# Joining the pairs of 128-column products in every step of an attention kernel: 50 fewer matmul calls

## The chip, the cores and the metric

The kernel runs on one core of a Trainium2 chip. The metric is the device time of one execution in microseconds (us), lower is better. Before the change it is 1023.34 us, the median of three runs (1022.62 to 1023.46).

## The reference, cut to what matters

```python
x: (64, 128, 512)   attn_bias: (16, 128, 128)   mask: (64, 128)   null_kv: (2, 64)     # float32
xn = layernorm(x, g_in)
q = (xn @ Wq).reshape(b, n, 16, 64).transpose(0, 2, 1, 3) * 64 ** -0.5
kv = xn @ Wkv                                   # one head of keys and values for all 16 query heads
k, v = kv[..., :64], kv[..., 64:]
k, v = null key ahead of k, null value ahead of v
sim = einsum('bhid,bjd->bhij', q, k) + bias     # causal and key mask
attn = softmax(sim, axis=-1)
out = einsum('bhij,bjd->bhid', attn, v)         # <- the products that the change joins
out = layernorm(out.transpose(0, 2, 1, 3).reshape(b, n, 1024) @ Wo, g_out)
return x + out
```

All is float32. A float32 matmul runs as two passes on TensorE (PE), each a weight load and a matmul, so one call in the code is four instructions on that engine.

## The kernel before, in words

64 batch elements are worked off in 32 pairs. The order of all work is written out by hand (`manual_schedule`): what stands first in the code stands first in its engine's stream. A step `d` is `turn(d)` and a body. `turn(d)` makes the scores of pair `d` (elements `a`, `b`), the attention-weighted values of the pair before (`p` and `p + 1`, with `p = 2d - 2`), and starts the softmax of `a`; the body has the key, query and output projections and the rest of the softmax. Steps 1 to 29 call `turn`, with `body` in steps 1 to 3 and `body_full` from 4; steps 30 to 32 call `turn_end`, which the change leaves alone.

On PE a step is three stretches: the scores (L780, 64 calls on 64x64 tiles of the array, into `sc_*` and `ps`), the values (L911, into `po`), and the body, mostly calls of 128x128 weights and 128 or 256 columns, which begins with `pkv` (L404). The values of one element are products of 32 keys: each of four groups of 32 queries (`s`) has its own 32 rows of the array, and each half of the heads (`r`) its own 64 columns, so eight tiles of the array work side by side. Causality leaves a group of queries only some blocks of keys. `sb` holds the transposed weights, six blocks of 32 by 32; of these `values` goes through four turns: the first has two blocks of a group in one call (256 columns), the next three have one each (128 columns). The argument `wide` names the groups (1 and 3) whose second and third turn are joined into one call of 256 columns:

```python
WIDE = (1, 3)
for turn in range(len(turns[0])):
    for s in range(NQ):
        j, to, n = turns[s % 2][turn]
        if s in wide and j == 1:
            if turn == 2:
                continue
            n = 2
        for r in range(2):
            nc.tensor.matmul(po[s][rows, to : to + n], vr[...], sb[quad, slots, ...], ...)
```

Without `wide` an element has 32 calls, with `WIDE[1:]` (group 3 alone) 30, with `WIDE` 28. In two steps from step 4 on, one of even and one of odd number, PE has 1536 instructions, its separate waits on semaphores counted. The results go from four tiles `po` in PSUM to `oT` by ScalarE (L930).

Of the kernel before, what the change touches and what calls it, by code (L numbers as in the profile page):

```python
# [17 lines left out]
def kernel(  # L18
# [515 lines left out]
    def token_sum(g, k):  # L534

        xS[g, k] = gp.tile([P, GB // 2, HK, N], FP, tag=f"xS{k}", name=f"xS{k}_{g}", bufs=1)
        lo, hi = xT[g][:, 0 : GB // 2], xT[g][:, GB // 2 :]
        b11, b12 = lo[:, :, lo_k], hi[:, :, lo_k]
        b21, b22 = lo[:, :, hi_k], hi[:, :, hi_k]
        p, m = {  # L540
            1: (b12, b11),
            2: (b22, xS.get((g, 1))),
            3: (b22, b12),
            4: (b21, xS.get((g, 2))),
        }[k]
        nc.gpsimd.tensor_tensor(xS[g, k], p, m, ALU.subtract)
# [182 lines left out]
    def mask_neg(g):  # L729
        m8 = m8s.pop(g).rearrange("p (t j) -> p t j", t=GB)  # L730
        for keys, m in ((LK, m8[:, :, 0:NL]), (UK, m8)):
            nc.scalar.activation(
                mneg[:, :, keys], m, AF.Identity, bias=neg, scale=-NEG
            )
# [3 lines left out]
    def bias_add(b, parts=(slice(0, ROW),)):  # L738
        g, t = divmod(b, GB)
        if b < B - 1:  # L740
            S[b] = sp.tile([P, R8, ROW], FP, tag="s", name=f"s_{b}", bufs=3)
        else:
            S[b] = hp.tile([P, R8, ROW], FP, tag="xb", name=f"s_{b}", bufs=1)
        for keys in parts:
            nc.gpsimd.tensor_tensor(  # L745
                S[b][:, :, keys],
                biasp[:, :, keys],
                mneg[:, t, keys]
                .unsqueeze(1)
                .broadcast_to([P, R8, keys.stop - keys.start]),  # L750
                ALU.add,
            )
# [12 lines left out]
    def scores(b, hf, tiles=None):  # L765
        g, t = divmod(b, GB)
        nk = N if hf == 1 else NL
        if tiles is None:
            whole = ps_s.tile([P, 2, NF * nk], FP, tag="s", name=f"ps_{b}_{hf}")
            whole = whole.rearrange("p r (f j) -> p r f j", f=NF)  # L770
            home = [whole[:, r] for r in range(2)]
            pss[b, hf] = whole
        else:
            home = rooms(b, hf, tiles)
            pss[b, hf] = home
        for f in range(NF):
            for r in range(2):
                rows = slice(r * DH, (r + 1) * DH)
                for u in range(2):
                    nc.tensor.matmul(  # L780
                        home[r][u * DH : (u + 1) * DH, f, :],
                        qT[g, f // 2, t // 2][rows, f % 2, t % 2, hf, u],
                        kT[rows, 0 : nk // Q, t, :],
                        start=True,
                        stop=True,
                    )
# [3 lines left out]
    def scores_add(b, hf):  # L790
        sv = S[b][:, :, KEYS[hf]].rearrange("p (r f) j -> p r f j", r=2)
        pv = pss.pop((b, hf))
        if isinstance(pv, list):
            for r in (1, 0):
                nc.vector.tensor_tensor(sv[:, r], pv[r], sv[:, r], ALU.add)  # L795
        else:
            nc.vector.tensor_tensor(sv, pv, sv, ALU.add)

    def scores_max(b, hf):
        if hf == 0:  # L800
            nmax[b] = small.tile([P, 2, R8], FP, tag="nmax", name=f"nmax_{b}")
        nc.vector.tensor_reduce(  # L802
            nmax[b][:, hf], S[b][:, :, WITH_NULL[hf]], AX.X, ALU.max, negate=True
        )

    def exps(b, hf, lo=0, hi=R8):
        if hf == 0 and lo == 0:
            rsum[b] = small.tile([P, 2, R8], FP, tag="rsum", name=f"rsum_{b}")
        for k in range(lo, hi):
            row = S[b][:, k, WITH_NULL[hf]]  # L810
            nc.scalar.activation(  # L811
                row,
                row,
                AF.Exp,
                bias=nmax[b][:, hf, k : k + 1],
                accum_out=rsum[b][:, hf, k : k + 1],
            )
# [38 lines left out]
    def values_rooms(  # L856
        p, rooms=((ps_q, "a"), (ps_w, "w"), (ps_y, "Y"), (ps_w, "w"))
    ):
        po = [
            pool.tile([P, 2, 2, NF, Q], FP, tag=tag, name=f"po_{p}_{s}")  # L860
            for s, (pool, tag) in enumerate(rooms)
        ]
        pos[p] = [t[:, :, 0] for t in po]
        pos[p + 1] = [t[:, :, 1] for t in po]
        return po
# [23 lines left out]
    WIDE = (1, 3)  # L889

    def values(b, wide=()):

        g, t = divmod(b, GB)
        sb = sbs.pop(b)
        po = pos[b]
        turns = (
            ((0, 0, 2), (1, 1, 1), (2, 1, 1), (3, 1, 1)),
            ((0, 0, 2), (1, 0, 1), (1, 1, 1), (2, 1, 1)),
# [8 lines that stand above are left out]
                quad = slice(s * Q, (s + 1) * Q)  # L907
                slots = slice(2 * to + j, 2 * to + j + 2 * n - 1, 2)
                for r in range(2):
                    rows = slice(r * DH, (r + 1) * DH)  # L910
                    nc.tensor.matmul(  # L911
                        po[s][rows, to : to + n],
                        vr[g][quad, t, PLACE[j], :],
                        sb[quad, slots, r * NF : (r + 1) * NF, :],
                        start=(turn == 0),
                        stop=True,
                        skip_group_check=(turn > 0),
                        tile_position=(s * Q, r * DH),
                    )
# [12 lines left out]
    def values_out(p, po):  # L932

        o = result_room(p)
        for s in range(NQ):
            u, i = divmod(s, 2)
            to = o[:, u].rearrange("p b f (s q) -> p s (b f) q", q=Q)[
                :, i : 4 - i : 3 - 2 * i
            ]
            add_null(to, po[s].rearrange("p s b f q -> p s (b f) q"), False)  # L940
# [148 lines left out]
    PAIRS = B // 2  # L1089
    late_T = []  # L1090

    def turn(d):

        a, b, p = 2 * d, 2 * d + 1, 2 * d - 2
        g = d // 2 + 1
        homes = (ps_y, "Y"), (ps_q, "a")
        if d == 1:
            homes = homes[::-1]
        scores(a, 0, (homes[0], (ps_w, "w")))
        scores(b, 0, (homes[1], (ps_w, "w")))  # L1100
        scores(a, 1)
        scores(b, 1, ((ps_y, "X"), (ps_q, "c")))
        scores_add(a, 0)
        scores_add(b, 0)
        scores_max(a, 0)
        scores_add(a, 1)
        scores_add(b, 1)
        po = values_rooms(p)
        steady = 3 < d < PAIRS - 2
        values(p, WIDE if steady else ())  # L1110
        values(p + 1, (WIDE if d % 2 else WIDE[1:]) if steady else ())
        if d % 2 and (d + 1) // 2 < NG:
            mask_neg((d + 1) // 2)
        bias_add(a + 2)
        if d % 2 == 0:
            token_sum(g, 1)
            token_sum(g, 2)
        exps(a, 0)
        values_out(p, po)
# [670 lines left out]
    for d in range(1, PAIRS - 2):  # L1790
        turn(d)
        (body_full if d > 3 else body)(d)
# [42 lines left out]
```

## Time and profile before

| What | Value |
|---|---|
| Median of three runs | 1023.34 us |
| The profiled execution's own time | 1022.45 us |
| Its span in the profile | 1020.6 us |
| PE busy (matmul) | 1012.9 us, 99% |
| PE weight loads busy | 902.0 us, 88% |
| VectorE, ScalarE, GpSimd busy | 860.8, 672.8, 775.0 us |
| Granted clock of PE | full in all 40 slices |
| Chain that ended last | PE 95%, ScalarE 2%, VectorE 1%, GpSimd 1% |
| Values (L911 into `po`) | 3700 matmuls |
| Instruction fetch of PE (queue q8) | 96 packets, 1.57 MB |

Rows of the timeline give the start of a group in us from the span's start, how long it lasts, the engine (PE matmul, PEld weight load), the line, the tiles (out <- in), the shape and the count. A row of windows gives the window, its length, the engine's busy time and the number of instructions in it, the granted clock, the DMA engines' busy share and GB/s. A row of waits says who waited for whom: us in total, times, longest. A row of a DMA queue gives packets, MB and the share of time of the 16 engines; in a window of some 0.02 us the share is over 100%, since a packet is counted whole where it starts.

### The profile page before, as it was taken

The numbers are of one execution on the slowest core, as the hardware profiler recorded it, in microseconds if no ns is written. First come the engines' busy times: TensorE is split into PE (matmuls) and PEld (weight loads), VectorE is DVE, ScalarE is ACT, GpSimd is POOL, SyncE is SP. The second block draws the span as 40 slices with busy tenths as digits, with TensorE's granted clock in tenths as the row PEclk, the third lists the DMA queues.
The fourth block names the chain that finished last, engine by engine and source line by source line (L and its number), as shares of the span: only waits on it lengthen the run. The fifth ranks groups of instructions, "written<-read, shape, count | busy, mean of one in ns | idle before, by whom it ended". The sixth has DMA issues, their size and how long they took to land.

```text
span 1020.6 us, 31143 instructions
## 1 busy us (share of the span) xinstructions
PE 1012.9 (99%) x12285; PEld 902.0 (88%) x12285; DVE 860.8 (84%) x1849; ACT 672.8 (66%) x2675; POOL 775.0 (76%) x621
## 2 busy tenths in 40 slices
PE   9999999999999999999999999999999999999997
PEld 9888888888888888888888888888888888888886
DVE  6877778888888988889888888888888888878787
ACT  5766677656677565686666776566765667856583
POOL 4997779678696876959768596785968769587686
PEclk9999999999999999999999999999999999999999
DMA  7415243151431425224152341514314152141221
GB/s 219 139 31 151 67 117 112 31 163 65 143 99 61 120 67 152 88 76 124 51 161 76 105 121 35 164 63 138 102 49 136 64 152 89 71 103 33 68 85 62
DMA packets 73833, 100.84 MB, mean 99 GB/s; under 512 B 32212, under 2 KB 36056, under 8 KB 71896
## 3 DMA queue, kind: packets, MB, share of 16 engines
q1 hardware_dynamic: 73392, 98.47, 32.3%
q8 instruction: 96, 1.57, 0.6%
q14 instruction: 49, 0.40, 0.1%
q10 hardware_dynamic: 296, 0.40, 0.1%
HBM read 63.19 MB, written 33.55 MB: 95 GB/s over the span
## 4 chain that ended last, share of the span: by engine, by line
PE 95%; ACT 2%; POOL 1%; DVE 1%; issue 0%; DMA 0%; POOLq 0%; DVEq 0%
PE pyX L998 20%; PE pa L603 13%; PE pi L697 11%; PE pyY L998 10%; PE po L911 8%; PE pkv L404 6%; PE pyw L998 5%; PE pc L603 4%; PE ps L780 3%; PE pq L499 3%; PE pa L554 2%; PE sc_X L780 2%; PE sc_Y L780 2%; PE pc L697 2%; ACT s L811 2%; PE pc L554 1%
## 5 line engine op out<-in xcount | busy, mean ns | idle before, releaser
L811 ACT ACTIVATE s<-s,nmax 128x65 f32<-128x65 f32 (+1 forms) x1024 | 370.9, 366 | 62.2 <-DVE nmax L802 62.2
L833 POOL TENSOR_TENSOR s<-s,rinv 128x512 f32<-128x512 f32 (+1 forms) x132 | 189.7, 1448 | 115.4 <-DVE rinv L829 112.9
L745 POOL TENSOR_TENSOR s<-biasp,mneg 128x1552 f32<-128x1552 f32 (+1 forms) x65 | 206.2, 3175 | 30.7 <-DVE s L795 21.2
L811 ACT ACTIVATION_READ_ACCUMULATOR s<-s,nmax 128x1 f32 x1024 | 194.5, 190 | 0.0
L725 DVE TENSOR_TENSOR qT<-pi,qT 128x128 f32<-128x128 f32 (+1 forms) x376 | 123.6, 340 | 35.9 <-PE pi L697 28.8
L1034 ACT COPY y<-pyX 128x256 f32<-128x256 f32 x29 | 10.8, 373 | 180.7 <-PE pyX L998 180.7
L802 DVE TENSOR_REDUCE nmax<-s 128x8 f32<-128x1032 f32 (+1 forms) x128 | 121.6, 950 | 0.1
L849 DVE STREAM_TRANSPOSE sb<-s 128x1536 f32<-128x1536 f32 (+1 forms) x68 | 113.6, 1674 | 2.1 <-POOL s L833 1.7
L998 PE MATMUL pyX<-wT,oT 128*128 128x256 f32 x464 | 109.7, 379 | 0.0
L998 PE MATMUL pyX<-wo,oT 128*128 128x256 f32 x464 | 109.7, 379 | 0.0
L978 POOL TENSOR_TENSOR oT<-oT 128x512 f32<-128x512 f32 x64 | 81.1, 1278 | 26.4 <-PE pyw L998 24.1
L998 PEld LDWEIGHTS pyX<-wT,oT 128*128 128x128 f32 x464 | 84.0, 190 | 9.2
L998 PEld LDWEIGHTS pyX<-wo,oT 128*128 128x128 f32 x464 | 84.0, 190 | 9.2
L911 PE MATMUL po<-sb,vr 32*64 32x128 f32 (+1 forms) x3700 | 86.2, 315 | 0.1
L911 PEld LDWEIGHTS po<-sb,vr 32*64 32x64 f32 x3700 | 74.8, 131 | 9.5 <-issue 5.3
L930 ACT ACTIVATE oT<-po,nv 128x512 f32<-128x512 f32 (+1 forms) x127 | 73.9, 660 | 0.4 <-PE po L911 0.4
L404 PE MATMUL pkv<-xT,wkv 128*128 128x256 f32 x256 | 63.3, 391 | 0.0
L998 PE MATMUL pyw<-wo,oT 128*128 128x256 f32 x256 | 60.5, 379 | 0.0
L998 PE MATMUL pyY<-wo,oT 128*128 128x256 f32 x256 | 60.5, 379 | 0.0
L998 PE MATMUL pyY<-wT,yS 128*128 128x256 f32 x256 | 60.5, 379 | 0.0
L614 ACT COPY qT<-pa 128x512 f32<-128x512 f32 x78 | 45.4, 582 | 17.7 <-PE pa L603 17.7
L404 PEld LDWEIGHTS pkv<-xT,wkv 128*128 128x128 f32 x256 | 46.2, 189 | 10.0 <-issue 4.8
(231 smaller groups left out, 2510.1 us busy)
## 6 DMA issues: line engine op xcount, KB each, us to landing
res<-in_x_dram SPq DMA_DIRECT2D x64, 256.0 KB
out_dram<-y SPq DMA_DIRECT2D x63, 256.0 KB
x<-in_x_dram SPq DMA_DIRECT2D x62, 256.0 KB
xd<-xb SPq DMA_DIRECT2D x14, 1024.0 KB
xT<-xd SPq DMA_DIRECT2D x56, 256.0 KB
vr<-vd SPq DMA_DIRECT2D x64, 128.0 KB
kT<-kT SPq DMA_DIRECT2D x32, 64.0 KB
vd<-vb SPq DMA_DIRECT2D x32, 64.0 KB
```

Of the source, the lines that this page charges most:

```text
L404: nc.tensor.matmul(pkv, wkv[:, kc, :], xT[g][:, t : t + 2, kc, :], start=(kc == 0), stop=(kc == KC - 1),)
L603: nc.tensor.matmul(prod[tag][:, i], w[:, kc, f * P : (f + 1) * P], t[:, :, kc, :], start=first, stop=(kc == HK - 1), skip_group_check=not ...
L697: nc.tensor.matmul(to, inner_w[k][i][:, h], inner_x[k, g][i], start=(i == 1), stop=True, skip_group_check=(i != 1),)
L725: nc.vector.tensor_tensor(o, p, o, ALU.add)
L745: nc.gpsimd.tensor_tensor(S[b][:, :, keys], biasp[:, :, keys], mneg[:, t, keys] .unsqueeze(1) .broadcast_to([P, R8, keys.stop - keys.start ...
L802: nc.vector.tensor_reduce(nmax[b][:, hf], S[b][:, :, WITH_NULL[hf]], AX.X, ALU.max, negate=True)
L811: nc.scalar.activation(row, row, AF.Exp, bias=nmax[b][:, hf, k : k + 1], accum_out=rsum[b][:, hf, k : k + 1],)
L833: nc.gpsimd.tensor_tensor(sv, sv, rinvs[b, hf][:, lo:hi].unsqueeze(2).broadcast_to([P, hi - lo, sv.shape[2]]), ALU.mult,)
L849: nc.vector.transpose(sbs[b][:, :, lo:hi].rearrange("p j e q -> p e j q"), S[b][:, lo:hi, 1 : ROW - 1].rearrange("p e (j k) -> p e j k", k=Q),
L911: nc.tensor.matmul(po[s][rows, to : to + n], vr[g][quad, t, PLACE[j], :], sb[quad, slots, r * NF : (r + 1) * NF, :], start=(turn == 0), st ...
L978: eng.tensor_tensor(o, a, b, op)
L998: nc.tensor.matmul(prod[key], h[:, c, :], w[:, c, :], start=(start and c == 0), stop=(c == HC - 1), skip_group_check=not start,)
```

## The change

Until now steps 1 to 3 joined no pair, and from step 4 to 29 the first element of a pair had both groups joined, the second both in odd steps and only group 3 in even ones. Now both groups are joined in both elements of every step.

```diff
@@ in turn(d)
         po = values_rooms(p)
-        steady = 3 < d < PAIRS - 2
-        values(p, WIDE if steady else ())
-        values(p + 1, (WIDE if d % 2 else WIDE[1:]) if steady else ())
+        values(p, WIDE)
+        values(p + 1, WIDE)
         if d % 2 and (d + 1) // 2 < NG:
```

On PE, in the values of the first element of step 1. The number behind `po_` is the group of queries, the next one a running number of the tile; `x2` are the two halves of the heads; `64x2x128` is a call of 256 columns:

```order
 L911 MATMUL po_3_857<-sb_662,vr_373 64x2x128 x2
 L911 MATMUL po_0_854<-sb_662,vr_373 64x128 x2
-L911 MATMUL po_1_855<-sb_662,vr_373 64x128 x2
+L911 MATMUL po_1_855<-sb_662,vr_373 64x2x128 x2
 L911 MATMUL po_2_856<-sb_662,vr_373 64x128 x2
-L911 MATMUL po_3_857<-sb_662,vr_373 64x128 x2
+L911 MATMUL po_3_857<-sb_662,vr_373 64x2x128 x2
 L911 MATMUL po_0_854<-sb_662,vr_373 64x128 x2
-L911 MATMUL po_1_855<-sb_662,vr_373 64x128 x2
 L911 MATMUL po_2_856<-sb_662,vr_373 64x128 x2
-L911 MATMUL po_3_857<-sb_662,vr_373 64x128 x2
```

Groups 1 and 3 take their second and third block in one call: two rows of two calls are gone, and as many for the second element, so that 32 instructions go in each of steps 1 to 3.

On PE, in the values of the second element of step 4, the first of the even steps with joined pairs, from its second turn to the first call of the body. Before:

```order
L911 MATMUL po_0_2003<-sb_1911,vr_1077 64x128 x2
L911 MATMUL po_1_2004<-sb_1911,vr_1077 64x128 x2
L911 MATMUL po_2_2005<-sb_1911,vr_1077 64x128 x2
L911 MATMUL po_3_2006<-sb_1911,vr_1077 64x2x128 x2
L911 MATMUL po_0_2003<-sb_1911,vr_1077 64x128 x2
L911 MATMUL po_1_2004<-sb_1911,vr_1077 64x128 x2
L911 MATMUL po_2_2005<-sb_1911,vr_1077 64x128 x2
L911 MATMUL po_0_2003<-sb_1911,vr_1077 64x128 x2
L911 MATMUL po_1_2004<-sb_1911,vr_1077 64x128 x2
L911 MATMUL po_2_2005<-sb_1911,vr_1077 64x128 x2
L911 MATMUL po_3_2006<-sb_1911,vr_1077 64x128 x2
L404 MATMUL pkv_2087<-xT_1815,wkv 128x256 x4
```

The same stretch after the change (the running numbers of the tiles are lower, since fewer instructions stand ahead):

```order
L911 MATMUL po_0_1979<-sb_1887,vr_1069 64x128 x2
L911 MATMUL po_1_1980<-sb_1887,vr_1069 64x2x128 x2
L911 MATMUL po_2_1981<-sb_1887,vr_1069 64x128 x2
L911 MATMUL po_3_1982<-sb_1887,vr_1069 64x2x128 x2
L911 MATMUL po_0_1979<-sb_1887,vr_1069 64x128 x2
L911 MATMUL po_2_1981<-sb_1887,vr_1069 64x128 x2
L911 MATMUL po_0_1979<-sb_1887,vr_1069 64x128 x2
L911 MATMUL po_1_1980<-sb_1887,vr_1069 64x128 x2
L911 MATMUL po_2_1981<-sb_1887,vr_1069 64x128 x2
L911 MATMUL po_3_1982<-sb_1887,vr_1069 64x128 x2
L404 MATMUL pkv_2061<-xT_1791,wkv 128x256 x4
```

One row of two calls is gone, eight instructions, in each of the 13 even steps from 4 to 28. Over the program PE has 50 calls, 200 instructions, fewer, and all that stands behind begins that much earlier in its stream. No other engine's work or order is changed.

## The prediction

> **What bounds the kernel now.** I read the page's busy times, the granted clock and the chain first, then PE's waits.
>
> ```profile
> PE 1012.9 (99%) x12285; PEld 902.0 (88%) x12285; DVE 860.8 (84%) x1849; ACT 672.8 (66%) x2675; POOL 775.0 (76%) x621
> PEclk9999999999999999999999999999999999999999
> PE 95%; ACT 2%; POOL 1%; DVE 1%; issue 0%; DMA 0%; POOLq 0%; DVEq 0%
> PE busy L1667 <- POOL neg L255: 1.4, 1, 1.4
> PE pyc L998 <- DVE y L1032: 0.6, 1, 0.6
> q8 instruction: 96, 1.57, 0.6%
> ```
>
> TensorE is the bound: 95% of the chain, a full clock, 2 us of waits in 1020.6. Whatever lengthens its stream lengthens the kernel, and nothing else does. The last row is used further down: 96 packets, 1.57 MB. A busy PE does not say how fast its stream moves, so I took the one stretch that is edited, the values block of a step, from the timeline: its first row's start, and the start of the row of `pkv` behind it. In order these are steps 1, 2, 3 (no joined pairs), 4 and 5 (116 and 112 matmuls), 28 and 29 (the last of 13 like step 4 and of 13 like step 5).
>
> ```profile
> 63.31 2.52 PE L911 MATMUL po<-sb,vr 32*64 32x256 f32 x128
> 65.76 0.48 PE L404 MATMUL pkv<-xT,wkv 128*128 128x256 f32 x1
> 94.70 2.65 PE L911 MATMUL po<-sb,vr 32*64 32x256 f32 x128
> 97.28 0.48 PE L404 MATMUL pkv<-xT,wkv 128*128 128x256 f32 x1
> 126.36 2.52 PE L911 MATMUL po<-sb,vr 32*64 32x256 f32 x128
> 128.81 0.48 PE L404 MATMUL pkv<-xT,wkv 128*128 128x256 f32 x1
> 157.58 2.63 PE L911 MATMUL po<-sb,vr 32*64 32x256 f32 x116
> 160.14 0.48 PE L404 MATMUL pkv<-xT,wkv 128*128 128x256 f32 x1
> 188.60 2.70 PE L911 MATMUL po<-sb,vr 32*64 32x256 f32 x112
> 191.23 0.48 PE L404 MATMUL pkv<-xT,wkv 128*128 128x256 f32 x1
> 902.78 2.63 PE L911 MATMUL po<-sb,vr 32*64 32x256 f32 x116
> 905.34 0.48 PE L404 MATMUL pkv<-xT,wkv 128*128 128x256 f32 x1
> 933.80 2.70 PE L911 MATMUL po<-sb,vr 32*64 32x256 f32 x112
> 936.44 0.48 PE L404 MATMUL pkv<-xT,wkv 128*128 128x256 f32 x1
> 157.57:188.59 31.02, 31.02 (x386) 1.00 0.25 79
> 188.59:219.68 31.08, 31.08 (x382) 1.00 0.43 120
> ```
>
> The block takes 2.45 us with 128 matmuls (steps 1 and 3; 2.58 in step 2), 2.56 with 116 and 2.63 with 112. Fewer, wider matmuls make it longer. The last two rows say that all of step 4, with 4 matmuls more, takes 31.02 us and step 5 takes 31.08.
>
> **The change, part one: the block itself.** Eight array tiles work at once, and a joined pair takes the time of two on its tile, so joining saves issues and no streaming; the rows show what the uneven turns cost. Steps 4, 6, … 28 go from the form of step 4 to that of step 5: 13 × 0.065 = 0.85 us. Steps 1, 2 and 3 go from 128 matmuls to 112: 3 × (2.63 − 2.45) = 0.55 us. Other engines are not moved, and PE waits for none of them. One early wait of the weight loads can swallow a little:
>
> ```profile
> PEld pc L554 <- DVE qT L592: 0.2, 1, 0.2
> ```
>
> It stands in step 2, so I take 0.2 us off. The rule that speaks for the change: the Trainium skill, Perfetto Trace Analysis, section Optimizing Tensor Performance, says that larger matmuls are more efficient than smaller ones where possible. By it 50 fewer calls would be a gain, the third rival below; the block rows do not bear it out.
>
> **Part two: where the instruction blocks begin.** The 12,285 matmuls and 12,285 weight loads over 96 packets of q8 make 256 instructions a packet, 16.4 KB each. 1536 is 6 × 256, so until now a block of 256 begins at the same place of every second step. The weight loads show such a place. First their starts in the stretch 0.28 to 0.44 us behind the first matmul of the values block, in steps 2, 3, 4, then of the blocks at 654.39 and 716.49 (two of the steps like 4); then when they go on in the first and fourth case:
>
> ```profile
> 94.98:95.14 0.16, 0.13 (x3) 1.00 0.21 77
> 126.64:126.80 0.16, 0.16 (x8) 1.00 0.00 0
> 157.86:158.02 0.16, 0.16 (x8) 1.00 0.27 102
> 654.67:654.83 0.16, 0.13 (x4) 1.00 0.27 102
> 716.77:716.93 0.16, 0.16 (x8) 1.00 0.28 102
> 95.31:95.64 0.33, 0.33 (x33) 1.00 0.26 93
> 654.82:654.97 0.15, 0.14 (x13) 1.00 0.22 82
> ```
>
> Twice the loads stop after three, and start again at 95.32 and 654.83, over 0.3 and 0.15 us late. Counted in the program, both stop before instruction 44 of the block, and those two instructions stand 13,826 = 54 × 256 + 2 apart: a new block of instructions begins there, and it was not in yet. The first time cost the 0.13 us by which step 2's block is longer than step 3's; the second cost nothing, the next matmul being due only at 0.50. The packets of q8, in windows 92.88:92.90, 154.96:154.98, 652.24:652.26 and 714.25:714.27, then 96.45:96.47 and 158.65:158.68:
>
> ```profile
> q8 instruction: 1, 0.02, 295.3%
> q8 instruction: 1, 0.02, 366.2%
> q8 instruction: 1, 0.02, 303.4%
> q8 instruction: 1, 0.02, 295.6%
> q8 instruction: 1, 0.02, 412.8%
> q8 instruction: 1, 0.02, 196.9%
> ```
>
> From 92.89 to 95.32 are 2.43 us and from 652.25 to 654.83 2.58; at 154.97 and 714.26 the packet started 2.9 and 2.5 us ahead of the same place, and nothing was late. So a block is usable 2.5 us after its packet starts. The fifth row starts 1.1 us after the late place: passing the start of one block asks for the next one. Together some 3.6 to 3.7 us must lie between the starts of two blocks. The sixth row, 158.66, less 1.1 is 157.56, when PE still ran about the last of the scores: it takes its instructions some 45 ahead of running them.
>
> A step has 768 instructions, and 480 to 490 of them are its scores and values. Of step 4, the first row of the scores and the first with 128 columns:
>
> ```profile
> 154.74 0.27 PE L780 MATMUL sc_Y<-kT,qT 64*64 64x64 f32 x2
> 155.72 1.06 PE L780 MATMUL ps<-kT,qT 64*64 64x128 f32 x32
> ```
>
> The 256 of the scores take 157.58 − 154.74 = 2.84 us (the first 128 0.98, 7.7 ns each, the others 14.5), so only here can two starts of blocks come too close. The other 280 of a step are spread over 25 us. Until now the two starts stand 36 to 44 instructions behind the first of the scores and behind the first of the values. Being 45 ahead, PE passes the first while the slow 128x256 matmuls of the body still run, and has the time: packet at 154.97, usable at 157.47, due at 157.86.
>
> The change takes 3 × 8 matmuls of 4 instructions out of steps 1 to 3 and 2 of 4 out of every second step. Both starts move back: to 76 in step 2, 105 in step 3, 138 and 140 in steps 4 and 5, and 8 more every two steps, 194 in step 18, 220 in step 25; from 226 (step 26) the second lies behind the values. The first is now passed among the quick scores. In step 4: when instruction 93 of the scores runs, 93 × 7.7 = 0.72 us; + 1.2 + 2.5 = 4.4, or 1.57 behind the first of the values; due there, by step 5's matmuls, at 1.45: 0.1 late. By the same sum 0.28 late in steps 2 and 3 (due at 0.79 and 1.06), 0 to 0.02 in steps 6 to 17, 0.04 to 0.17 in 18 to 25 (of the scores the later half now counts, at 14.5 ns), nothing from 26 on. Packets come earlier or later in equal steps: of the three of steps like 4 above they start 2.61, 2.13 and 2.23 us ahead of the values' first matmul, ±0.24 about the middle. Early ones gain nothing, so the mean over the 24 steps from 2 to 25 is about 0.13 us: 3.1 us. This is the term that I know least. Its lower end is 0, as in the block at 654.39, where the lateness was covered; below 0 it cannot go but for the 0.13 us of step 2, since nothing is late elsewhere. Its upper end is another 0.15 us in each of 24 steps, half of what step 2 showed: 6.7 us. I take 3.1, worked out from the nearest rows, those of the same blocks. In steps 30 to 32, written in another order, the starts move by 200 instructions; by step 2 that is up to 0.3 us at three places, gained or lost, and I take 0.
>
> The sum: 0.85 + 0.55 − 0.2 + 3.1 − 0.13 (step 2's old lateness) = +4.2 us. The profiled execution took 1022.45 us, 1.85 more than its span, and becomes 1026.7. The runs' median, 1023.34, is 0.9 above it: 1027.5.
>
> **Rivals.**
> First: the new starts of blocks are hidden. The estimate of lateness in steps 6 to 17 is so near 0 that 0.15 us less leaves 1 us of it. For this speaks the block at 654.39; against, step 2 and that 24 steps must all be lucky. Only part one is left: +1.1, 1024.4, which a measurement of this kernel cannot tell from no change (0.2%, 2.05 us, is about its limit). The Trainium skill, Runtime: NRT & Kernel Launch, section Instruction fetch mechanics, would have it so: PE's instruction memory is refilled in blocks of 256 instructions, and crossing into the next is mostly hidden. The trace agrees with the 256 and shows two crossings that were not hidden.
> Second: each start costs more, since a stop also breaks the order in which the eight tiles turn: 24 × 0.28, all steps like step 2's new place, is 6.7, with part one 8: above 1030.
> Third, the other sign: fewer calls pay. Two matmuls of 128 columns last 2 × 270 ns, one of 256 lasts 390:
>
> ```profile
> L911 PE MATMUL po<-sb,vr 32*64 32x256 f32 x1380 | 72.7, 390 | 0.1
> L911 PE MATMUL po<-sb,vr 32*64 32x128 f32 x2320 | 67.7, 270 | 0.0
> ```
>
> 50 calls of two passes would save 100 × 150 ns on eight tiles, 1.9 us, and with step 2's lateness gone 2.0: 1021.3. It decides if a block of 112 matmuls is shorter than one of 116; the block rows say the opposite 26 times of 26.
> That the count does not change is excluded: 50 matmuls are gone from the built order.
>
> **How the numbers follow.** Forecast (1025.4 to 1030) 0.62; hidden starts 0.18; dearer starts 0.17; fewer calls pay 0.03. Time 1027.5. The range leaves out the third rival, the luckiest of the first and the worst of the second: 1024.4 to 1031.5. Slower by over 0.2% are the forecast and the second rival, 0.79; within 0.2% the first, 0.18; faster 0.03.
>
> **What would show it.** The values block of every step from 1 to 29 at 2.63 us or more, none at 2.45 or 2.56; steps 26 to 29 at 2.63 like step 5 now, since no start of a block falls in it; steps 2 and 3 the longest of the early ones, 2.9; stretches with few weight loads, later in the block from step to step; body and scores unchanged. PE's waits stay near 2 us and its clock full. The forecast is wrong if the blocks of steps 6 to 25 are 2.63 to the hundredth (first rival) or if 2.9 is the rule (second), and my reading of q8 is wrong if long blocks come where no start of a block falls.

## The result, and the profile after

The changed kernel takes 1030.1 us (median of 6 runs, 1028.62 to 1031.34), the kernel before on the same chip 1023.18 (6 runs, 1022.62 to 1023.46): a ratio of 1.0068, 95% interval 1.0055 to 1.0081, 6.9 us slower. The forecast was 1027.5, 4.2 us slower, with a range from 1024.4 to 1031.5. The profiled execution took 1029.69 us with a span of 1027.8; before it was 1022.45 and 1020.6, so the two traces differ by 7.2 us and can be compared block by block.

The page after: busy times, granted clock, chain, and the queue of instructions.

```profile
PE 1017.3 (99%) x12185; PEld 904.0 (88%) x12185; DVE 859.1 (84%) x1849; ACT 674.3 (66%) x2675; POOL 775.3 (75%) x621
PEclk9999999999999999999999999999999999999999
PE 95%; ACT 1%; DVE 1%; POOL 1%; issue 1%; DMA 0%; POOLq 0%; DVEq 0%
q8 instruction: 96, 1.57, 0.6%
```

TensorE has 100 matmuls fewer (50 calls of two passes) and is busy 4.4 us longer. Clock and chain stay as they were; "issue", time in which an engine waits for nothing that the profile shows, goes from 0% to 1% of the chain. The bodies of the steps are unchanged within 0.01 us, but for 0.04 us less in step 2. The loss is all in the scores, the values and the first call behind the values.

The values blocks of steps 2, 5, 16 and 28, each with its first row and the row of `pkv` behind it (start, duration):

```profile
95.00 2.70 PE L911 MATMUL po<-sb,vr 32*64 32x256 f32 x112
97.63 0.48 PE L404 MATMUL pkv<-xT,wkv 128*128 128x256 f32 x1
189.17 2.93 PE L911 MATMUL po<-sb,vr 32*64 32x256 f32 x112
192.03 0.48 PE L404 MATMUL pkv<-xT,wkv 128*128 128x256 f32 x1
532.46 3.12 PE L911 MATMUL po<-sb,vr 32*64 32x256 f32 x112
535.51 0.70 PE L404 MATMUL pkv<-xT,wkv 128*128 128x256 f32 x2
909.25 2.70 PE L911 MATMUL po<-sb,vr 32*64 32x256 f32 x112
911.88 0.48 PE L404 MATMUL pkv<-xT,wkv 128*128 128x256 f32 x1
```

From the first start to that of `pkv`: 2.63, 2.86, 3.05 and 2.63 us. All blocks have 112 matmuls now and 2.63 is their length where nothing is late. Step 2, late before, is no longer; steps 5 and 16 are. After minus before, block by block, in us:

| what | where | sum |
|---|---|---|
| form of the values block | steps 1, 3: +0.18 each; step 2: +0.05; 13 even steps from 4: +0.075 each | 1.39 |
| late, within the values | step 5: 0.22; 6: 0.06; 7: 0.23; 13: 0.05 | 0.57 |
| late, in the scores of even steps | 16: 0.76; 20: 0.83; 22: 0.10; 28: 0.25 | 1.94 |
| late, in the values of even steps | 16: 0.42; 20: 0.85; 22: 0.50 | 1.76 |
| late, behind the values | 26: 0.78 | 0.78 |
| late, in step 30 | the second stretch of scores, 1.03 to 1.76 | 0.72 |
| start-up | | 0.1 |

That is 7.26. "Late" is what a stop at a start of a block adds to a step. The prediction's form is there, its late starts are dearer (5.8 for 3.1), and three fifths of them (3.44 us) stand where it had put none: in the scores, behind the values of step 26, in step 30.

**The costly ones, read from step 16.** PE in the scores of step 16: the first row, the first with 128 columns, and the one after a stop.

```profile
528.86 0.27 PE L780 MATMUL sc_Y<-kT,qT 64*64 64x64 f32 x2
529.84 1.04 PE L780 MATMUL ps<-kT,qT 64*64 64x128 f32 x29
531.22 0.32 PE L780 MATMUL ps<-kT,qT 64*64 64x128 f32 x2 [0.34 <-issue]
```

The loads of weights (PEld) ahead of the stop, in it and behind it: 11 in 0.20 us, then 5 in 0.67, then 10 in 0.18.

```profile
530.30:530.50 0.20, 0.20 (x11) 1.00 0.33 106
530.53:531.20 0.67, 0.12 (x5) 1.00 0.26 92
531.22:531.40 0.18, 0.17 (x10) 1.00 0.30 102
```

At 531.22 the stream passes a start of a block: instruction 188 of the scores, by the count of the program. Its packet is in the next three views: the bytes in the window 521.5 to 528.59 by queue, the same for 528.59 to 528.60, and the row of DMA shares over 518 to 532 (one digit is 0.35 us).

```profile
q1 hardware_dynamic: 993, 1.59, 96.6%
q8 instruction: 1, 0.02, 678.8%
DMA  9899970000396589999999999999999944322222
```

528.59 to 531.22 are 2.63 us, as the prediction had it (2.43 to 2.58). But what asked for this packet was not a start in the scores or the values: it was the third start of the step, which PE passed in the body of step 15, at 522.47. The packet went 6.1 us later. From 521.5 to 528.59 the 16 DMA engines were 96.6% busy with q1 alone, and the packet went 0.6 us before they came free, at 529.2 in the last row. What filled them, from SP's issues:

```profile
520.62 1.76 SPq L384 DMA_DIRECT2D xT<-xd  x4
522.42 0.90 SPq L141 DMA_DIRECT2D res<-in_x_dram  x2
523.36 1.15 SPq L132 DMA_DIRECT2D x<-in_x_dram  x2
524.97 1.70 SPq L447 DMA_DIRECT2D vd<-vb  x2
```

The tokens of a group come once in two steps, 4 × 256 KB, with 4 × 256 KB of `res` and `x` behind them, always in the body of an odd step; hence only even steps have late scores. In step 13 the same start, 8 instructions earlier, was passed at 459.85; its packet had gone at 458.17, just ahead of the transfers (PE reads its instructions some way before it runs them), and nothing was late. From step 15 on the request falls into the transfers: the third packets of steps 15, 19, 21, 23, 25 and 27 go 6.1, 4.8, 3.8, 3.1, 2.4 and 2.3 us after their start was passed, each 0.6 to 1.2 us before the engines come free (step 27's ahead of a second batch). Only step 17's slipped through in the middle, after 1.6 us, and step 18 was on time. In the kernel before, the third start of step 15 lay 144 instructions further ahead, and its packet went 4 us before it was passed.

One such packet can be paid for twice. In steps 16, 20, 22 and 26 the packet for the start behind it, in or just behind the values, went 1.1 to 1.4 us after the start in the scores was passed; in the odd steps from 15 to 27 this was 0.2 to 0.5 us. A block that comes late seems to leave PE no lead in asking for the next; this is read from the times, and no run tests it alone. These are the 1.76 us within the values and the 0.78 us behind them. The page puts step 26's stop down to VectorE:

```profile
L404 PE MATMUL pkv<-xT,wkv 128*128 128x256 f32 x256 | 63.3, 391 | 0.7 <-DVE rinv L829 0.7
```

But `rinv` ended at 849.03 and `pkv` went on only at 849.45; in the kernel before the same call began ahead of `rinv`. Its first weight load is the first instruction behind a start of a block, whose packet went at 846.58, 2.87 us earlier, so it is counted as late here.

### The profile page after: what moved, and what is told of

It is laid out like the page before. It is cut to its first block, busy times and chain, and to the rows that moved or that the text cites. A ratio compares the mean times of both kernels' runs of the same rounds, so it can differ in the third digit from the quotient of the medians.

```text
span 1027.8 us, 30943 instructions
## 1 busy us (share of the span) xinstructions
PE 1017.3 (99%) x12185; PEld 904.0 (88%) x12185; DVE 859.1 (84%) x1849; ACT 674.3 (66%) x2675; POOL 775.3 (75%) x621
## 4 chain that ended last, share of the span: by engine, by line
PE 95%; ACT 1%; DVE 1%; POOL 1%; issue 1%; DMA 0%; POOLq 0%; DVEq 0%
PE pyX L998 20%; PE pa L603 13%; PE pi L697 10%; PE pyY L998 10%; PE po L911 8%; PE pkv L404 6%; PE pyw L998 5%; PE pc L603 4%; PE pq L499 3%; PE ps L780 3%; PE pa L554 2%; PE sc_X L780 2%; PE sc_Y L780 2%; PE pc L697 2%; ACT s L811 1%; PE pc L554 1%
## 5 line engine op out<-in xcount | busy, mean ns | idle before, releaser
L911 PE MATMUL po<-sb,vr 32*64 32x128 f32 (+1 forms) x3600 | 89.0, 320 | 1.1 <-issue 0.9
```

Source lines behind the costliest of these rows:

```text
L911: nc.tensor.matmul(po[s][rows, to : to + n], vr[g][quad, t, PLACE[j], :], sb[quad, slots, r * NF : (r + 1) * NF, :], start=(turn == 0), st ...
```

## The experiments

Times are medians; each is compared with the kernel before on the same chip (1022.98 to 1023.29). "Extra" is the length of a step's scores or values block above that of the same form where nothing is late, summed over one trace.

**1. The kernel before, its starts moved.** 24 calls of the early part are split in two, 96 instructions in all; count, form and steps stay.

```diff
-        q_mm(pq, c, h)
+        if h == 1 and c < 6:
+            q_mm(pq, c, h, slice(0, 1))
+            q_mm(pq, c, h, slice(1, 2))
+        else:
+            q_mm(pq, c, h)
```

> The kernel before, no pair joined beyond its own, 1536 instructions for two steps as before. Only the place of the block starts is moved, by 24 calls of the early queries split into two of half the columns (96 instructions more ahead of step 1): they stand 204 (even steps) and 197 (odd) behind the first of the scores, where they stand in steps 18 to 20 after the change. Theory of the starts: the even steps lose what steps 20 and 22 lost after the change, 0.6 to 1.7 us each, 13 of them: 1031 to 1045 us, and the values blocks that are not late keep 2.56 and 2.63. Rival, the joined calls themselves cost the time: 1023.2 + 0.4 for the split calls, 1023.6. Rival, it is the drift from step to step and not the place: 1023.6 too.

1035.41 us, ratio 1.0121 (1.0104 to 1.0138). No values block changed its form, and it is 12.4 us slower: place alone costs. The extra is 3.97 us in scores and 8.11 in values, all but 0.7 of it (steps 1 and 2) in even steps. The third start has the same place here in each odd step, and so in each even one: in the 12 odd steps from 5 to 27, with the tokens' transfers, the packet goes 3.9 to 4.7 us after the start is passed, in the 13 even steps from 4 to 28, without them (the engines some 22% busy around the start of step 6), 1.3 to 2.0 us before.

**2. The changed kernel with the same 96 instructions**, so that its starts drift from 44 to 148 instead of from 138.

> The change as it is, all pairs joined and the count of two steps 1528, so that the starts drift as before by 8 every two steps; but the same 96 instructions more ahead of step 1, so that they go from 44 (step 4) to 148 (step 30) and never come to 186 to 236. Theory of the starts: only the form of the blocks is left, 1.4 us, and 0.4 for the split calls, with up to 0.5 us of small lateness: 1025 to 1025.5 us; values blocks 2.63. Rival, joined calls cost the time: 1030.5. Rival, drift: 1030.5.

1029.52 us, ratio 1.0065 (1.0050 to 1.0080): not what was expected. The late scores are gone (extra 0.09 us), but the values are late by 0 to 0.7 us a step, 3.7 in all, 3.2 of it from step 16 on. So the other mechanism, two starts too close in scores and values, costs several us too where it applies.

**3. The changed kernel with its loads of `x` earlier** in the odd steps.

```diff
+        if m + 2 < B and xw and h == 1:
+            load_x(m + 2)
+            load_x(m + 3)
...
-        if m + 2 < B and xw:
+        if m + 2 < B and xw and h == 0:
```

> The change as it is; only the two loads of x in odd steps from step 5 on are issued at the start of the body and no longer behind the token transfer, so that the full stretch of the DMA engines ahead of the next even step ends about 2 us earlier. Theory that the packet of the next block waits behind these transfers: in steps 16, 20, 22, 24, 26 and 28 the packet starts 2 us earlier and the block is there in time: most of the 4.5 us lost there come back, 1025.5 to 1027 us. Rival, the packet waits for a semaphore of PE's own stream, not for the DMA engines: same as the change, 1030.

1031.48 us (1027.29 to 1033.86), ratio 1.0081 (1.0055 to 1.0106). A miss, and one that decides nothing: the tokens' transfers stay, the engines are busy until 529.2 as before, and step 16's packet went 0.14 us ahead of its scores again. The edit took away the wrong half of the transfers.

**4. The form alone**: all four pairs joined in the even steps, the 8 instructions put back by two split calls of `kv_pair`, starts where they were.

```diff
-        values(p + 1, (WIDE if d % 2 else WIDE[1:]) if steady else ())
+        values(p + 1, WIDE if steady else ())
...
-        pkv = kv_pair(g * GB + 2 * h)
+        pkv = kv_pair(g * GB + 2 * h, halves=(1, 2) if h == 0 else ())
```

> The kernel before with one part of the change: the second element of the even steps from 4 on has both groups joined too. The 8 instructions that this takes out are put back by splitting two of the key-value calls of 256 columns in two of 128, so that two steps have 1536 and every start of a block stays where it was, but for those two instructions' distance. Theory: form alone, 13 x 0.075 us, and 13 x 0.02 for the split calls: 1024.4 us, even values blocks 2.63. Rival, fewer and larger calls pay when the starts stay: 1022.5. Rival, the joined calls cost all of the 7 us: 1028 or more.

1024.57 us, ratio 1.0014 (1.0004 to 1.0023), 1.6 us slower. In steps 1 to 29 no block is late but step 2's (0.14). In the trace, whose span is 1.9 us longer, the form is 13 × 0.075 = 0.98 us, the prediction's first term; the split calls add 13 × 0.03 = 0.39, one late start in step 31 0.33 and the start-up 0.15. That the time lies by the first rival's 1024.4 is a coincidence, since steps 1 to 3 are not joined here.

**5. Other orders in the block.** The kernel before, each step's block issued in another order, all with their old count.

> The kernel before, with its count and its starts of blocks, but the values block of each step from 1 to 29 issued in another order or with another one of its four pairs left apart: 13 orders of 112 matmuls in the odd steps, 13 of 116 in the even ones, 3 of 128. Theory A (the joined calls cost because the last turns on the eight tiles become uneven): orders that spread both elements' joined calls ahead of the narrow ones come down from 2.63 towards the 2.45 of the block with no joined pair; orders that only permute the strips inside a turn stay at 2.63 +-0.05. Theory B (a wide call costs for itself): every order of 112 stays at 2.63 and every one of 116 at 2.56, within 0.03. Whole run: within 4 us of the kernel before.

1023.63 us, a single execution. The blocks of step 5 (order as before), step 11 (joined calls last in the second element), step 15 (all wide calls first), step 17 (strips in the order 0, 2, 1, 3), then step 26 (116 matmuls, the strips also 0, 2, 1, 3), with the last one's `pkv`:

```profile
188.66 2.70 PE L901 MATMUL po<-sb,vr 32*64 32x256 f32 x112
375.25 2.63 PE L901 MATMUL po<-sb,vr 32*64 32x256 f32 x112
499.50 2.89 PE L901 MATMUL po<-sb,vr 32*64 32x256 f32 x112
562.08 2.52 PE L901 MATMUL po<-sb,vr 32*64 32x256 f32 x112
841.63 2.52 PE L901 MATMUL po<-sb,vr 32*64 32x256 f32 x116
844.08 0.48 PE L404 MATMUL pkv<-xT,wkv 128*128 128x256 f32 x1
```

To `pkv` these are 2.63, 2.56, 2.82, 2.45 and 2.45 us. Theory B falls, since orders of the same 112 calls differ by 0.37 us; theory A had the wrong orders, since spreading the wide calls over both elements gave 2.62 to 2.64, or 2.82, and permuting the strips, which was to change nothing, gave 2.45, the length of the block with no pair joined. Not every permutation does: 1, 3, 0, 2 gave 2.65, and 0, 2, 1, 3 with the two elements' turns alternating gave 2.61. Each order stands in one step only; experiment 9 repeats the best one.

**6. The changed kernel without the tokens' transfers.** Groups 2 to 15 use the tokens of group 1. TensorE's matmuls are the same; with the transfers goes one semaphore instruction in two steps, so the starts drift a little otherwise: the third of step 15 is instruction 219 of the body, not 211.

```diff
     def tokens_in(g):
-        ...
+        xT[g] = xT[1]
```

> The changed kernel without the four transfers of 256 KB that fetch the tokens of groups 2 to 15 (all groups use the tokens of group 1), TensorE's instructions unchanged. Theory A (the packet of a block of instructions queues behind these transfers): the late starts of the even steps 16, 20, 22, 26 and 28 go, 4.2 to 4.5 us; the small ones of steps 1 to 7 and the one of step 30 stay: 1025.3 to 1026.3. Theory B (they are late because TensorE asks too late, whatever the transfers do): as the changed kernel, 1029 to 1031.

1028.04 us (1026.86 to 1030.05), ratio 1.0051 (1.0036 to 1.0066): the time is between the two theories, the trace is not. The third start of step 15 is passed at 524.30. Its packet is in the window 526.11 to 526.12, and step 16's first scores and first values are on time:

```profile
q8 instruction: 1, 0.02, 855.0%
529.83 0.27 PE L773 MATMUL sc_Y<-kT,qT 64*64 64x64 f32 x2
532.67 2.70 PE L904 MATMUL po<-sb,vr 32*64 32x256 f32 x112
```

1.8 us after the start, where it had been 6.1, and between 1.6 us before and 1.8 after it in all odd steps from 13 to 27, which go through the places of the changed kernel's steps 15 to 27. The scores take 2.84 us again in every step, where 1.94 us were lost. What was missed: the values are late by 2.26 us in all, 0.3 to 0.5 in steps 4, 6, 8 and 22. In step 4 the packet asked for in the scores goes 0.48 us before the values' first matmul; in the changed kernel 1.1. Without the tokens, the transfers that fill `vr` come earlier. SP's issue of them around step 4, in this kernel and in the changed one:

```profile
155.54 1.73 SPq L445 DMA_DIRECT2D vr<-vd  x4
```

```profile
162.47 1.74 SPq L452 DMA_DIRECT2D vr<-vd  x4
```

At 155.54 they run into the scores of step 4. So here, as far as one step shows it, taking one load from the engines let another meet the packets.

**7. Experiment 1 without the tokens' transfers.**

> The kernel of the first experiment (the kernel before, its starts of blocks moved to 197 and 204 in every step, 1035.4 us) without the four transfers that fetch the tokens of a group. Theory A (packets queue behind these transfers): of the 12 us of late starts, all in even steps, three quarters or more go: 1023.5 to 1027. Theory B (TensorE asks too late): 1033 to 1036.

1027.25 us, ratio 1.0041 (1.0026 to 1.0056): 8.2 of the 12.4 us of experiment 1 are gone, two thirds where three quarters were expected, and again all of the scores' part (3.97 to 0.0); the values' part falls from 8.11 to 4.24, 1.26 of that in step 2. The third packets of the odd steps from 5 to 27, which in experiment 1 went 3.9 to 4.7 us after the start was passed, go from 1.5 us before to 1.3 us after it. With 6, this shows that packets of instructions wait behind data.

**8. The pairs of steps 1 to 3 alone**: a single shift by 96, then 1536 for two steps again.

```diff
-        values(p, WIDE if steady else ())
-        values(p + 1, (WIDE if d % 2 else WIDE[1:]) if steady else ())
+        values(p, WIDE)
+        values(p + 1, WIDE[1:] if steady and d % 2 == 0 else WIDE)
```

> The kernel before with the joined pairs of steps 1 to 3 alone: 24 matmuls fewer once, the count stays 1536 for two steps, and the starts of blocks stand 96 earlier, at 133 and 140 of the scores and of the values, from step 4 on; the third lies some 120 instructions ahead of the next scores, ahead of the transfers. Theory A (late are pairs of starts too close, by 0 to 0.25 us a step as steps 4 and 5 of the changed kernel show, and packets behind the transfers, which this place avoids): 0.5 from the form and 26 steps of 0.05 to 0.15: 1024.8 to 1027.5, no late start over 0.4 us. Theory B (only the old place is safe, each other one costs by chance 0.3 to 1.2 in the even steps as in the first experiment): above 1029.

1029.36 us, ratio 1.0063 (1.0046 to 1.0080), above what theory A gave and where theory B had it. The scores are clean in all steps (extra 0.0), as they should be with the third start ahead of the transfers. The values are late by 5.5 us in all, about 0.2 a step. Step 15, one of the middle ones:

```profile
501.44 3.01 PE L911 MATMUL po<-sb,vr 32*64 32x256 f32 x112
504.39 1.78 PE L404 MATMUL pkv<-xT,wkv 128*128 128x256 f32 x7
```

2.94 us for 2.63. The packet went 1.1 us after the start in the scores was passed, and 0.6 to 1.4 us in the other steps; the longest, 1.4, is in step 16, the latest block of all (0.94 us), where the transfers of the odd step end only in the scores. The engines are 0.9 busy or more at that place in the other even steps from 10 on too, and step 26 still lost nothing (its packet went after 0.6 us). So the same place costs 0 in some steps and 0.9 in another, and full engines alone do not tell which.

**9. The kernel before with strips 0, 2, 1, 3** where pairs are joined.

```diff
-            for s in range(NQ):
+            for s in (0, 2, 1, 3) if wide else range(NQ):
```

> The kernel before, with the four strips of each turn taken in the order 0, 2, 1, 3 where pairs are joined (the ones with joined pairs last); count and starts of blocks unchanged. Theory A (by the trace of the orders: 2.453 us with 112 and with 116 matmuls, where 0, 1, 2, 3 gave 2.632 and 2.560): 13 x 0.179 + 13 x 0.107 = 3.7 us less, 1019.2 to 1020.2. Theory B (the single blocks of that run were a chance of their place, or the shorter block uncovers its start of a block in steps 4 to 28): 1021.5 to 1023.5.

1019.79 us (1019.01 to 1020.18), ratio 0.9968 (0.9956 to 0.9981): 3.2 us faster than before, and faster than both kernels. Its page:

```profile
span 1017.0 us, 31143 instructions
PE 1009.0 (99%) x12285; PEld 898.3 (88%) x12285; DVE 860.7 (85%) x1849; ACT 672.5 (66%) x2675; POOL 775.2 (76%) x621
```

The same instructions, and a span of 1017.0 for 1020.6. All blocks of steps 4 to 29 take 2.45 us; none is late but step 2's, by 0.13.

**10. The changed kernel with that order.**

> The changed kernel with the same order of strips: every values block of 112 comes to 2.453, so nothing is left of the form's cost, 29 x 0.18 = 5.2 us, while count and starts of blocks are as in the changed kernel. Theory A (form and late starts add up): 1030.1 - 5.2 = 1024.9, with the late starts drawn anew and the blocks due up to 0.1 us earlier: 1024 to 1027, so still slower than the kernel before, and 4 us or more above the same order with the old starts. Theory B (late starts come from the uneven turns themselves, a stop breaking the order in which the tiles turn): as that kernel, 1019 to 1021.

1027.47 us (1027.07 to 1029.44), ratio 1.0043 (1.0027 to 1.0058), 7.7 us above experiment 9. Every block that is not late takes 2.45 us, so the form costs nothing any more, and what is left between the two kernels is the moved starts. The values of step 16 in this kernel:

```profile
531.13 2.31 PE L911 MATMUL po<-sb,vr 32*64 32x256 f32 x93
534.15 0.65 PE L911 MATMUL po<-sb,vr 32*64 32x128 f32 x19 [0.71 <-issue]
534.73 1.56 PE L404 MATMUL pkv<-xT,wkv 128*128 128x256 f32 x6
```

3.60 us for 2.45. The third start of step 15 was passed at 520.97 and its packet went 6.3 us later, at 527.23. Theory B, that the uneven turns make the late starts, is out: they are as dear without them. The median is half a microsecond above theory A's range and 2.6 us below the changed kernel, where the form gave 5.2: the other half went into more late starts. The profiled execution shows them, though it was the slowest of the four (1029.44 us): 10.2 us in steps 1 to 29, against 5.1 in the changed kernel. That faster blocks meet their starts earlier is a likely reason, not a shown one.

## Why the prediction was right, and where its sizes were off

- **What bounds the kernel.** Right: TensorE's stream, its clock full, its waits for other engines as before but for the 0.7 us that the page books on `rinv`. Everything lost was lost in its own stream.
- **The form, +0.85 + 0.55 − 0.2.** Right in kind: with step 2's old lateness (−0.13), which the prediction booked apart, its sum is 1.07, and the trace has 1.39. The even steps gave 0.98 and not 0.85, since the rows differ by 0.07 to 0.08 us a step and not by 0.065; of the 0.2 taken off for the weight loads' wait step 2's body shows 0.04. The reading of 112 against 116 and 128 matmuls held in every block. What the prediction did not see is that the price belongs to the order of the strips and not to joining: experiments 5 and 9.
- **The rule that larger matmuls are more efficient** (the Trainium skill, Perfetto Trace Analysis, section Optimizing Tensor Performance), the third rival: no run bears it out here. In the best order 112, 116 and 128 matmuls take 2.45 us each, in the order of the kernel the fewest take longest.
- **A block is usable 2.5 us after its packet, and asked for when the start before it is passed.** Right: 2.63 us in step 16, 2.25 to 2.95 over the late starts of this trace. Experiment 1 shows the cost of place with nothing else changed.
- **The late starts, +3.1.** The mis-sized term: 5.8 us in the trace, 5.5 by the medians (6.9 less 1.4), 7.7 between experiments 10 and 9. The step that failed stands in "so only here can two starts of blocks come too close. The other 280 of a step are spread over 25 us". The third start, in the body, was taken to be harmless since it has time. It has 6 us, and the transfers take them. With it failed "nothing from 26 on" and "body and scores unchanged": step 26 lost 0.78 us behind the values, and the scores of four even steps lost 1.94, 0.25 of it in step 28.
- **"Packets come earlier or later in equal steps", ±0.24.** Wrong in kind. The packet of the same start goes 1.3 to 2.0 us before it is passed in even steps, and up to 4.7 us after it in odd ones behind the tokens (experiment 1), 6.1 and 6.3 us after it in step 15 of the changed kernel and of experiment 10. The sum by places also failed step by step: steps 2 and 3, called the longest of the early ones with 2.9, took 2.63, as their packets went 0.8 and 0.9 us after the instruction 45 ahead of the start ran, where the sum had 1.2; steps 5 and 7 took 2.86. The mean of 0.13 a step for 24 steps was not far off by its size for what it described, 0.2 in experiment 8, but in the changed kernel it hit other steps.
- **Steps 30 to 32, taken as 0** with up to 0.3 at three places: step 30 lost 0.72, a stop of the kind shown above.

```profile
974.03 0.28 PE L780 MATMUL sc_Y<-kT,qT 64*64 64x128 f32 x2
974.82 0.32 PE L780 MATMUL sc_Y<-kT,qT 64*64 64x128 f32 x2 [0.41 <-issue]
975.19 1.99 PE L998 MATMUL py_s<-wo,oT 128*128 128x256 f32 x8
```

- **Hidden starts, the first rival.** The changed kernel is not its 1024.4, but thirteen of the twenty steps from 6 to 25 lost nothing, as this rival had it for all. The Trainium skill, Runtime: NRT & Kernel Launch, section Instruction fetch mechanics, says that crossing into the next 256 instructions is mostly hidden. By count that holds, most of the 96 starts cost nothing; by time it does not, since a dozen of them cost 5.8 us.
- **Dearer starts, the second rival.** By the time alone it is level with the forecast: 1030.1 is just past the forecast's 1030 and in its "above 1030". Its pattern is not there: it had 0.28 us in every step, and the loss is 0.6 to 1.7 us in steps 16, 20 and 22 and nothing in most others. That a stop also breaks the order in which the tiles turn is not shown by any run.
- **The sign of the sum** was carried by the form and a rough term that could only be positive. The forecast came out 2.6 us too low. It lies inside its range only because that range had been drawn to half of step 2's lateness more in each of 24 steps, not because the mechanism that filled it was in it: that part of the hit is luck.

What stays open: why the order 0, 2, 1, 3 is free and 0, 1, 2, 3 is not; why in the odd steps of experiments 2 and 8 the packet needs 0.5 to 1.2 us after the start in the scores, though the engines carry next to nothing meanwhile; and why in the even steps of experiment 8, with full engines, it needs hardly longer, 0.6 to 1.4 us, where the tokens' transfers cost 4 to 6 us in the body.

## What to carry to other kernels

When a kernel is bound by one engine's stream, count its instructions modulo the block in which they are fetched before and after an edit: a change of 50 calls moved the starts of blocks in 30 steps, and that cost four times what the calls themselves did. Look for late starts as stretches with few weight loads and no releaser, or with one that had ended before, and then look at what the DMA engines carry between the passing of the start before and the packet: instructions wait behind data. And before calls are joined to save some, try the order in which they are issued; here it was worth more than the joining, in one line and with the count left alone.

## What was not expected of the hardware

- A packet of instructions has a queue of its own but no right of way: in odd steps of experiment 1 it went 3.9 to 4.7 us after the start before it was passed, behind transfers that fill the 16 engines, and without the tokens' transfers (experiment 7) at most 1.3 us after it.
- Late starts go with scatter. The kernel before, with its starts in a safe place, ran within 0.84 us over six runs, and within 0.9 to 1.8 over seven to thirteen on other chips; the changed one ran within 2.7 over six, the experiments with moved starts within 1.8 (the second) to 6.6 (the third) over four each.
- The order of four strips in a turn moves a block of the same 112 matmuls between 2.45 and 2.65 us (experiment 5), with no wait that any row shows.
